# Image 0's value planes: column-mod-4 order from PSUM, eight rows at a time on ScalarE and GpSimd

## The chip, the cores and the metric

The program runs on one core of a Trainium2 chip, in one launch. Its engines are TensorE (PE, matrix products into PSUM), VectorE (DVE), ScalarE (ACT), GpSimd (POOL) and SyncE (SP, which here only issues DMAs); ACT and POOL issue some DMAs as well. PE's weight loads are listed as PEld. The metric is the device time of one execution in microseconds (us).

## The reference

The kernel computes two layers on x of shape (4, 96, 128, 128), fp32. Layer 0 is a state-space block (projection, 3x3 depthwise convolution, four scans, a norm, an output projection). Layer 1, cut to what matters:

```python
x1, x2 = split at zero and normalized from _gn(x)          # per image, 96 x 128 x 128 each
key   = conv3x3(x1, aw1);  qry = conv3x3(x2, aw2)
attn  = softmax over (c, 3x3) of the products of key and qry patches   # 96 x (96*9) per image
value = conv3x3(x1, aw3)
y1    = layer_norm(conv3x3(value, attn))                   # each image has its own filter attn
y2    = layer_norm(conv3x3(x2, w_conv2)) * x1
x     = x + xr + conv1x1(concat(y1, y2), w_full) + b_full
```

## The kernel before

The program is emitted by Python generators that run in pairs: co_run steps a left generator and a right one, at a given ratio of their costs. A scheduler then places the instructions on the engines' queues; each engine and each DMA queue works through its own list in order.

The order of stages: projections and scans of all four images; from about 2550 us on, beside the rest of the scan, image 0's convolutions (direct_maps); from about 3290 us on, when the scan has ended, the same convolutions beside image 1's norm and split; then the attention of images 0 to 3, each beside the norm and split of the next image and the output of the last one.

**The convolutions of image 0** (direct_maps, pair_sets). They work on plain rows, three at a time, in bank-sized PSUM tiles of psl (three of them). There are 22 strips of six rows; in each, m = 0 makes key and value from x1d, m = 1 makes query and the other convolution from x2d. For each m, two chunks of three rows give 128 output channels (96 of key or query, and 32 of the value or other), and one product of 2 x 64 channels the rest. convolve evicts each PSUM tile with ACT copies (L2116). The 32 channels go to the ring and from there to DRAM (last_32, L1783); the 64 channels go to the tile value or o and from there to DRAM (first_64, L1800). For m = 0 the DRAM tensor is vd, rows of 129 columns with a leading zero.

**Image 0's value planes.** The attention multiplies transformed inputs: each row is cut in tiles of four columns, and six linear combinations of six neighbouring columns make the planes vp. For images 1 to 3 the value is made in column-mod-4 order on the chip. For image 0, lift reads rows of vd back (L2143) into a padded tile and pixel_planes makes the planes on DVE: 12 instructions per four rows (L1428 to L1437) with steps of four columns. store_planes writes them to vp (L1444). lift is called after every strip with the number of rows that are surely there, and makes at most four lifts then; once more with all rows after the attention's weights are made:

```python
for _ in range(4 if rows < H else H // LR):
    a = lifted[0]
    if not img.lifting or a + LR > rows:
        return
```

img.lifting becomes true when the scan has ended.

**The other helper for planes.** planes_of serves images whose rows lie in column-mod-4 order, 33 places for each of the four residues (PP = 132 a row, the last place of each zero). With vector=True it works on DVE (L1380 to L1387, and L1373); otherwise ACT makes two scaled copies x4 and x2 (L1394, L1395), and POOL ten sums and differences (L1403 to L1408, and four of L1373). Image 1's split uses both forms, one for x1p and one for x2p, after DVE's selection L1230 of what ACT scaled (L1226).

**Image 1's norm** (ssm_output, 16 steps). It runs on all engines beside the convolutions: PE L950 and L1002 into banks of psr (two of them), DVE L1015 and L1021, POOL L1016, two small DMAs in POOL's queue (L988 writes a row rd, L996 spreads it out as r).

**After the convolutions.** Taps.weights makes the softmax (L1692, L1694), PE transposes it (L1703), DVE copies it (L1704) and transforms the filter (L1265 to L1271); it is stored as watd and read back as wa by ACT's queue (L1337 to L1343). Attention.load reads ya and yc from the planes (L1880, L1888), ACT copies parts as yb (L1905), and products multiplies them (L1471).

Of the kernel before, what the change touches and what calls it, by code (L numbers as in the profile page):

```python
# [9 lines left out]
F32 = mybir.dt.float32  # L10
BF16 = mybir.dt.bfloat16
AF = mybir.ActivationFunctionType
ALU = mybir.AluOpType
# [4 lines left out]
C = 96  # L18
# [16 lines left out]
PP = PB * TW  # L35
AA = 2.0
AR = 12
LR = 4
GROUP = 9
NG = H // GROUP  # L40
NSTRIP = (H + AR - 1) // AR
# [28 lines left out]
def kernel(  # L70
# [1168 lines left out]
    def turned_view(v):  # L1239

        return v.rearrange("p (h t j) -> p h j t", t=TN, j=TW)
# [101 lines left out]
                eng.dma_start(w3[p : p + 32, j], wd[64:96, 2, i])  # L1343
        return w1, w2, w3

    def padded(t, r):


        v = t[:, : r * PP].rearrange("p (h w) -> p h w", w=PP)
        nc.gpsimd.memset(v[:, :, W + 1 : PP], 0.0)  # L1350
        nc.gpsimd.memset(v[:, :, 0:1], 0.0)
        nc.gpsimd.memset(t[:, r * PP :], 0.0)
        return v[:, :, 1 : W + 1]

    def planes_of(later, pool, t, r, then, most=RS, vector=False, bufs=2, p=C):


# [52 lines left out]
            later(lambda: then(pl), 2)  # L1410

        return at_once if vector else scaled

    def pixel_planes(later, pool, t, r, then):

        v = t[:, : r * PP].rearrange("p (h x) -> p h x", x=PP)

        def x(k):  # L1420
            return v[:, :, k : k + W - TW + 1 : TW]

        def made():
            f = pool.tile([C, 6, r, TN], F32, name="diff", bufs=1)
            pl = pool.tile([C, NP, r * TN], F32, name="pl")
            stt = nc.vector.scalar_tensor_tensor
            for k in range(TW):
                stt(f[:, k], x(k), -AA * AA, x(k + 2), ALU.mult, ALU.add)  # L1428
            for k in (1, 2):
                nc.vector.tensor_sub(f[:, 3 + k], x(k + 2), x(k))  # L1430
            to = [pl[:, i].rearrange("p (h t) -> p h t", t=TN) for i in range(NP)]
            nc.vector.tensor_sub(to[0], f[:, 2], f[:, 0])
            nc.vector.tensor_sub(to[5], f[:, 3], f[:, 1])
            nc.vector.tensor_add(to[1], f[:, 2], f[:, 1])
            nc.vector.tensor_sub(to[2], f[:, 2], f[:, 1])
            for i, a in ((3, AA), (4, -AA)):
                stt(to[i], f[:, 4], a, f[:, 5], ALU.mult, ALU.add)  # L1437
            later(lambda: then(pl))

        return made  # L1440

    def store_planes(eng, m, r0, r, pl):
        to = m[:, :, r0 + 1 : r0 + 1 + r].rearrange("c i h t -> c i (h t)")
# [129 lines left out]
    def by_threes(v, r):  # L1573

        return v.rearrange("p (i q) w -> p i q w", q=min(3, r))
# [191 lines left out]
                    lambda ks=ks, groups=groups: self.multiplied(s == 0, ks, *groups)  # L1767
                )

    def last_32(img, m, v, c0, r, k):  # L1770

        r0, r = r

        def f():
            if m:
                for i in range(v.shape[1]):
                    nc.vector.bn_stats(img.c2a[96:128, k + i], v[96:128, i])
                to = img.c2d[64:96, r0 * W : (r0 + r) * W]
            else:
                to = img.vd[64:96, (r0 + 1) * PW : (r0 + 1 + r) * PW]  # L1780
            to = to.rearrange("c (h w) -> c h w", h=r)
            for i in range(v.shape[1]):
                nc.sync.dma_start(to[:, 3 * i : 3 * i + v.shape[2]], v[96:128, i])  # L1783

        return f

    def first_64(img, m, t, parts, chunks, k):


        def f():  # L1790
            if m:
                for p, e, v, _ in parts:
                    for i in range(v.shape[1]):
                        nc.vector.bn_stats(img.c2b[p:e, k + i], v[:, i])
            for q, (r0, r) in enumerate(chunks):
                if m:
                    to = img.c2d[0:64, r0 * W : (r0 + r) * W]
                else:
                    to = img.vd[0:64, (r0 + 1) * PW : (r0 + 1 + r) * PW]
                nc.sync.dma_start(to, t[64 * q : 64 * q + 64, : to.shape[1]])  # L1800

        return f

    def pair_sets(img, taps, later, pool, rows, inputs, convolve, lift):

        value = pool.tile([128, rows * PW], F32, name="value", bufs=1)
        nc.gpsimd.memset(value.rearrange("p (h w) -> p h w", h=rows)[:, :, 0:1], 0.0)
        c = 0  # L1810
        per = rows // 3
        for s, chunks in enumerate(strips_of(rows)):
            for m in (0, 1):
                read = []
                for q, (r0, r) in enumerate(chunks):
                    read.append(inputs(c, q))
                    c += 1
                    jobs = [(0, 128, 0, read[q], r * W)]
                    to = [(0, 128, taps.rows(m, r0, r, 1), r)]
                    v = taps.rows(m, r0, r, 1 if m else 0)  # L1820
                    then = last_32(img, m, v, 0, (r0, r), per * (2 * s + q))
# [6 lines left out]
                v = t.rearrange("p (h w) -> p h w", h=rows)  # L1828
                if not m:
                    v = v[:, :, 1:PW]  # L1830
                rs = [r for _, r in chunks]
                if rs == [rows, rows]:
                    to = [(0, 128, by_threes(v, rows), rows)]
                else:
                    to = [
                        (64 * i, 64 * i + 64, by_threes(v[64 * i : 64 * i + 64, :r], r), r)
                        for i, r in enumerate(rs)
                    ]
# [220 lines left out]
    def direct_maps(img, ps):  # L2059
# [3 lines left out]
        with (  # L2063
# [32 lines left out]
            def convolve(jobs, m, to, then):  # L2096
                pc = bank(ps)
                for i, (k, d) in enumerate(terms):
                    for p, e, c, t, n in jobs:
                        v = t[k][:, d : d + n // W * PW].rearrange("p (h w) -> p h w", w=PW)  # L2100
                        w = ws[m][k][:, d] if k < 2 else ws[m][2]
                        nc.tensor.matmul(  # L2102
                            pc[p:e, :n].rearrange("p (h w) -> p h w", w=W),
                            lhsT=w[:, c : c + e - p],
                            rhs=v[:, :, 0:W],
                            start=(i == 0),
                            stop=(i == len(terms) - 1),
                        )
                    if i in (2, 4, 6):
                        later.tick()  # L2110
                        yield 2.1 if i == 2 else 1.4

                def out():
                    for p, e, v, r in to:
                        of = pc[p:e, : r * W].rearrange("p (h w) -> p h w", w=W)
                        nc.scalar.copy(v, by_threes(of, r))  # L2116
                    later(then)

                later(out)
# [8 lines left out]
            def lift(rows):  # L2128
# [5 lines that stand above are left out]
                    if not lifts:  # L2134
                        lifts.append(
                            pools.enter_context(tc.tile_pool(name="lifts", bufs=2, side="left"))
                        )
                    lifted[0] = a + LR
                    h = lifts[0].tile([C, LR * PP + 4], F32, name="lift")
                    to = padded(h, LR)  # L2140
                    src = img.vd[:, (a + 1) * PW : (a + LR + 1) * PW]
                    src = src.rearrange("c (h w) -> c h w", w=PW)
                    nc.sync.dma_start(to, src[:, :, 1:PW])  # L2143
                    later(pixel_planes(
                        later, lifts[0], h, LR, lambda pl, a=a: store_planes(nc.sync, img.vp, a, LR, pl)
                    ), 2)
                    yield 1.2

# [303 lines left out]
    with tc.tile_pool(name="wp", bufs=1, side="left") as wp:  # L2452
# [7 lines left out]
        for images, pace in (([0], 0.25), ([1], 0.75), ([2, 3], 1.35)):  # L2460
            left = projections(images, weights, stats, wp, psl)
            if images[0] == 0:
# [3 lines left out]
                next(made)  # L2466
                while ready[0] < 2:
                    next(left)
                maps = [new_map(n) for n in ("x1d", "x2d", "vd")]
                planes = [  # L2470
                    [new_planes(f"{n}{i}") for n in ("x1p", "x2p", "vp")] for i in range(2)
                ]
# [154 lines left out]
```

## Time and profile before

| what | value |
|---|---|
| runs of the kernel | 6656.29 us median of three, 6639.72 to 6660.51 |
| the profiled execution | 6633.8 us; span from the first to the last instruction 6631.9 us |
| mean granted TensorE clock | 0.886 |
| busy share of the span | PE 81%, PEld 35%, DVE 74%, ACT 57%, POOL 53% |
| instructions | 76453 |

A busy share is an average over stages that have different limits, so the stages around the change are to be read one by one. In the views, "<-" in front of a name says what an idle engine was waiting for; an entry such as "DVE diff L1430" names the engine, the tile and the line. Groups give the count after x, the busy us, the mean ns of one, and the idle time before. A view of one tile gives the shortest, median and longest duration in ns and the first and last start in us.

### The profile page before, as it was taken

Reading aid. Unit: us, or ns where it says so; the run is one execution under the profiler, and the core shown is the slowest. Engines: PE = TensorE matmul, PEld = TensorE weight load, DVE = VectorE, ACT = ScalarE, POOL = GpSimd, SP = SyncE. Lnnn points to the kernel's source line nnn. Section 1 sums busy time; section 2 is a strip of 40 time slices with the busy share of each in tenths; the row PEclk is TensorE's granted clock in tenths of the full one; section 3 lists DMA queues with packets and bytes.
Section 4 is the critical chain, followed back from the end, with each engine's and each line's share of the span. In section 5 each row is a group of like instructions: output and inputs, shape, how many; then the busy total and the mean of one; then the engine's idle time right before and its main releaser. Section 6 shows DMA issues by size and latency. Waiting matters only on the chain. (4 is left out here: it accounts for less than half of the span.)

```text
span 6631.9 us, 76453 instructions
## 1 busy us (share of the span) xinstructions
PE 5374.8 (81%) x23264; PEld 2337.9 (35%) x23264; DVE 4907.7 (74%) x7469; ACT 3803.6 (57%) x4751; POOL 3506.9 (53%) x2744
## 2 busy tenths in 40 slices
PE   5889988987887736989987479877888777887988
PEld 2333323322222102444433134444333444344553
DVE  3247778988997568989755885588875788898666
ACT  1257768777786566676534464475544654545542
POOL 2236758978787436969621354466234574034320
PEclk9999989998997757999998789987988887998989
DMA  7766777866765667665666765655775555866547
GB/s 165 174 155 181 201 206 198 223 192 163 222 182 162 187 171 213 198 199 170 203 184 177 195 182 156 174 143 157 206 202 155 147 154 154 227 173 188 150 122 213
DMA packets 888487, 1198.29 MB, mean 181 GB/s; under 512 B 216143, under 2 KB 741015, under 8 KB 875597
## 3 DMA queue, kind: packets, MB, share of 16 engines
q1 hardware_dynamic: 864460, 1138.46, 63.1%
q0 software_dynamic: 16208, 38.42, 2.2%
q10 hardware_dynamic: 7408, 16.53, 0.8%
q8 instruction: 187, 3.06, 0.2%
q14 instruction: 224, 1.83, 0.1%
HBM read 777.62 MB, written 345.58 MB: 169 GB/s over the span
## 5 line engine op out<-in xcount | busy, mean ns | idle before, releaser
L622 PE MATMUL bank<-y,wp 128*128 128x512 f32 (+3 forms) x3584 | 1316.6, 624 | 85.5 <-DMA y<-y 34.4
L855 POOL TENSOR_TENSOR y<-y,dl 128x1024 f32<-128x1024 f32 x384 | 1056.4, 2751 | 272.1 <-DVE dl L847 238.0
L822 POOL TENSOR_TENSOR dl<-dl,u 128x1024 f32<-128x1024 f32 x384 | 1009.2, 2628 | 223.6 <-ACT dA L798 107.5
L843 DVE TENSOR_TENSOR_SCAN dA<-dA,pBC 128x512 f32<-128x512 f32 x768 | 981.5, 1278 | 30.7
L1471 PE MATMUL two<-ya,wd 128*64 128x192 f32 (+3 forms) x2376 | 595.1, 427 | 193.5 <-ACT odd L1542 96.8
L847 DVE TENSOR_TENSOR dl<-dA,pBC 128x512 f32<-128x512 f32 x768 | 528.0, 688 | 271.4 <-PE pBC L736 198.5
L736 PE MATMUL pBC<-xr,wbc 60*128 60x512 bf16 (+1 forms) x1536 | 458.8, 403 | 330.0 <-DVE dA L843 257.7
L622 PEld LDWEIGHTS bank<-y,wp 128*128 128x128 f32 (+3 forms) x3584 | 458.8, 169 | 754.2 <-issue 655.5
L2102 PE MATMUL bank<-y,wn 128*128 128x384 f32 (+5 forms) x2408 | 676.8, 504 | 43.0 <-DMA y<-x2d 18.9
L1905 ACT COPY yb<-ya 64x768 f32<-64x768 f32 (+1 forms) x660 | 537.8, 815 | 152.0 <-PE two L1471 111.7
L665 ACT ACTIVATE dl<-pd,dtb 128x512 f32<-128x512 f32 x768 | 485.6, 684 | 181.2 <-PE pd L736 171.3
L1471 PE MATMUL two<-yb,wd 128*64 128x192 f32 (+3 forms) x2376 | 567.6, 411 | 21.3 <-ACT yb L1905 21.3
L826 DVE TENSOR_TENSOR pBC<-dl,pBC 128x512 f32<-128x512 f32 x768 | 527.5, 687 | 9.7 <-POOL dl L822 8.8
L2102 PEld LDWEIGHTS bank<-y,wn 128*128 128x128 f32 (+3 forms) x2408 | 307.5, 167 | 338.9 <-issue 165.4
L798 ACT ACTIVATE dA<-dl,negA 128x1024 f32<-128x1024 f32 x384 | 420.3, 1141 | 2.3
L1471 PEld LDWEIGHTS two<-ya,wd 128*64 128x64 f32 (+1 forms) x2376 | 268.9, 172 | 405.4 <-ACT odd L1542 104.0
L736 PEld LDWEIGHTS <-wbc 60*128 60x128 bf16 (+1 forms) x1536 | 103.4, 96 | 767.7 <-issue 754.0
L665 ACT ACT_TABLE_LOAD x245 | 314.3, 1283 | 100.9 <-PE pd L736 93.6
L1975 POOL COPY own<-ring 32x512 f32<-32x512 f32 (+1 forms) x198 | 225.3, 1172 | 260.7 <-DVE ring L1564 224.4
L1471 PEld LDWEIGHTS two<-yb,wd 128*64 128x64 f32 (+1 forms) x2376 | 294.0, 173 | 167.5 <-issue 37.3
L2209 POOL MEMSET o<- 1x1024 f32 x60 | 56.3, 946 | 560.3 <-PE bank L2264 225.3
L1471 PE MATMUL two<-ya,wa 128*96 128x384 f32 (+1 forms) x528 | 230.1, 519 | 123.3 <-DMA ya<-vp 82.5
(323 smaller groups left out, 9936.6 us busy)
## 6 DMA issues: line engine op xcount, KB each, us to landing
u<-zb SPq DMA_DIRECT2D x192, 1024.0 KB
yms<-y SPq DMA_DIRECT2D x96, 512.0 KB
y<-yms SPq DMA_DIRECT2D x64, 768.0 KB
xn<-xnew SPq DMA_DIRECT2D x128, 384.0 KB
ya<-vp SPq DMA_DIRECT2D x120, 336.0 KB
y<-y SPq DMA_DIRECT2D x128, 258.2 KB
zb<-z SPq DMA_DIRECT2D x64, 512.0 KB
ya<-x1p SPq DMA_DIRECT2D x90, 336.0 KB
```

The source lines that it names most:

```text
L622: nc.tensor.matmul(blocks(pz[p:e]), lhsT=ws[k][:, d, c : c + e - p], rhs=window(ys[k], at, d, n), start=(i == 0), stop=(i == len(terms) - 1),)
L665: nc.scalar.activation(dst, src, AF.Softplus, bias=bias)
L736: nc.tensor.matmul(p, lhsT=w[rows], rhs=xr[rows, at : at + CH], start=True, stop=True)
L798: nc.scalar.activation(live[m]["dA"], live[m]["dl"], AF.Exp, scale=negA[:, g % 3, k : k + 1])
L822: nc.gpsimd.tensor_mul(t, t, u_view(n))
L826: nc.vector.tensor_mul(p, live[n]["dl"][:, bass.ts(half, CH)], p)
L843: nc.vector.tensor_tensor_scan(h, h, p, init, ALU.mult, ALU.add)
L847: nc.vector.tensor_mul(live[n]["dl"][:, sl], live[n]["dA"][:, sl], live[n]["C", half])
L855: nc.gpsimd.tensor_add(v, v, t.rearrange("p (a b) -> p a b", b=W))
L1471: nc.tensor.matmul(of(to[p:e], r), lhsT=w[:, i, c : c + e - p], rhs=tiles(t[k][PAIR[i]][:, SLOT[i]], o, r), start=(k == 0), stop=False,)
L1905: nc.scalar.copy(yb[k][64 * h - 64 : 64 * h, :, :n], ya[k][0:64, :, h * TN : h * TN + n])
L2102: nc.tensor.matmul(pc[p:e, :n].rearrange("p (h w) -> p h w", w=W), lhsT=w[:, c : c + e - p], rhs=v[:, :, 0:W], start=(i == 0), stop=(i == ...
```

## The change

The value of image 0 leaves PSUM in column-mod-4 order. The 96 query or key channels are evicted as before, and for m = 0 the 32 value channels get an ACT copy of their own into one of two places of a new tile, whose borders are cleared once; the 64 channels go in the same order to the tile value. vd becomes rows of 132 places with the borders in them, so each store is one run per channel. lift reads eight rows (LR = 8) as one run per channel and calls planes_of in its ACT and POOL form with one buffer each for x4, x2 and the planes; pixel_planes and padded go.

```diff
-LR = 4
+LR = 8
...
+    def turned_rows(t, r):
+        return t[:, : r * PP].rearrange("p (h j b) -> p h j b", j=TW, b=PB)[:, :, :, 0:TN]
...
     def last_32(img, m, v, t, r, k):
...
             if m:
...
             else:
+                nc.sync.dma_start(
+                    img.vd[64:96, r0 * PP : (r0 + r) * PP], t[:, : r * PP]
+                )
...
-        value = pool.tile([128, rows * PW], F32, name="value", bufs=1)
+        value, end = (
+            pool.tile([128, rows * PP], F32, name=f"value{i}", bufs=1) for i in range(2)
+        )
+        ends = end[96:128], end[64:96]
...
-                    to = [(0, 128, taps.rows(m, r0, r, 1), r)]
+                    if m:
+                        to = [(0, 128, v, r)]
+                    else:
+                        to = [(0, 96, v[0:96], r), (96, 128, turned_rows(ends[q], r), r)]
...
-                        of = pc[p:e, : r * W].rearrange("p (h w) -> p h w", w=W)
-                        nc.scalar.copy(v, by_threes(of, r))
+                        of = pc[p:e, : r * W]
+                        if list(v.shape[2:]) == [TW, TN]:
+                            of = turned_view(of)
+                        else:
+                            of = by_threes(of.rearrange("p (h w) -> p h w", w=W), r)
+                        nc.scalar.copy(v, of)
...
-                    h = lifts[0].tile([C, LR * PP + 4], F32, name="lift")
-                    to = padded(h, LR)
-                    src = img.vd[:, (a + 1) * PW : (a + LR + 1) * PW]
-                    src = src.rearrange("c (h w) -> c h w", w=PW)
-                    nc.sync.dma_start(to, src[:, :, 1:PW])
-                    later(pixel_planes(
-                        later, lifts[0], h, LR, lambda pl, a=a: store_planes(nc.sync, img.vp, a, LR, pl)
+                    h = lifts[0].tile([C, LR * PP], F32, name="lift")
+                    nc.sync.dma_start(h, img.vd[:, a * PP : (a + LR) * PP])
+                    later(planes_of(
+                        later, lifts[0], h, LR,
+                        lambda pl, a=a: store_planes(nc.sync, img.vp, a, LR, pl), LR, bufs=1,
                     ), 2)
...
-                maps = [new_map(n) for n in ("x1d", "x2d", "vd")]
+                maps = [new_map(n) for n in ("x1d", "x2d")]
+                maps.append(dram.tile([C, H * PP], F32, name="vd", bufs=1))
```

The helper that is called now, in the form that lift takes:

```python
def scaled():
    x4 = pool.tile([p, most * PP], F32, name="x4", bufs=bufs)[:, : r * PP]
    x2 = pool.tile([p, most, 2, PB], F32, name="x2", bufs=1)[:, :r]
    nc.scalar.mul(x4, t[:, : r * PP], a2)
    nc.scalar.mul(x2, v.rearrange("p h (k b) -> p h k b", b=PB)[:, :, 0:TW:2], AA)
    later(lambda: differences(x4.rearrange("p (h x) -> p h x", x=PP), x2))
```

More of the change, by code (lines that the diff above doesn't have):

```diff
@@ L1344, in product_stack @@
         return w1, w2, w3
[L1346 to L1353, printed above, removed]
     def planes_of(later, pool, t, r, then, most=RS, vector=False, bufs=2, p=C):
@@ L1412, in planes_of @@
         return at_once if vector else scaled
[L1414 to L1440, printed above, removed]
     def store_planes(eng, m, r0, r, pl):
@@ L1768, in complete, with last_32 @@
                 )
-    def last_32(img, m, v, c0, r, k):
+    def turned_rows(t, r):
+        return t[:, : r * PP].rearrange("p (h j b) -> p h j b", j=TW, b=PB)[:, :, :, 0:TN]
+    def last_32(img, m, v, t, r, k):
         r0, r = r
@@ L1775, in f @@
             if m:
+                to = img.c2d[64:96, r0 * W : (r0 + r) * W].rearrange("c (h w) -> c h w", h=r)
                 for i in range(v.shape[1]):
                     nc.vector.bn_stats(img.c2a[96:128, k + i], v[96:128, i])
-                to = img.c2d[64:96, r0 * W : (r0 + r) * W]
+                    nc.sync.dma_start(to[:, 3 * i : 3 * i + v.shape[2]], v[96:128, i])
             else:
[L1780 to L1783, printed above, removed]
+                nc.sync.dma_start(
+                    img.vd[64:96, r0 * PP : (r0 + r) * PP], t[:, : r * PP]
+                )
         return f
@@ L1795, in f @@
             for q, (r0, r) in enumerate(chunks):
[L1796 to L1800, printed above, removed]
+                to, n = (img.c2d, W) if m else (img.vd, PP)
+                nc.sync.dma_start(
+                    to[0:64, r0 * n : (r0 + r) * n], t[64 * q : 64 * q + 64, : r * n]
+                )
         return f
     def pair_sets(img, taps, later, pool, rows, inputs, convolve, lift):
-        value = pool.tile([128, rows * PW], F32, name="value", bufs=1)
-        nc.gpsimd.memset(value.rearrange("p (h w) -> p h w", h=rows)[:, :, 0:1], 0.0)
+        value, end = (
+            pool.tile([128, rows * PP], F32, name=f"value{i}", bufs=1) for i in range(2)
+        )
+        ends = end[96:128], end[64:96]
+        for t in (value, end):
+            nc.gpsimd.memset(t, 0.0)
         c = 0
@@ L1818, in pair_sets @@
                     jobs = [(0, 128, 0, read[q], r * W)]
-                    to = [(0, 128, taps.rows(m, r0, r, 1), r)]
-                    v = taps.rows(m, r0, r, 1 if m else 0)
-                    then = last_32(img, m, v, 0, (r0, r), per * (2 * s + q))
+                    v = taps.rows(m, r0, r, 1)
+                    if m:
+                        to = [(0, 128, v, r)]
+                    else:
+                        to = [(0, 96, v[0:96], r), (96, 128, turned_rows(ends[q], r), r)]
+                    then = last_32(img, m, v, ends[q], (r0, r), per * (2 * s + q))
                     yield from convolve(jobs, m, to, then)
@@ L1827, in pair_sets @@
                 t = pool.tile([128, rows * W], F32, name="o3") if m else value
[L1828 to L1838, printed above, removed]
+                to = []
+                for i, (_, r) in enumerate(chunks):
+                    v = t[64 * i : 64 * i + 64]
+                    if m:
+                        v = by_threes(v[:, : r * W].rearrange("p (h w) -> p h w", w=W), r)
+                    else:
+                        v = turned_rows(v, r)
+                    to.append((64 * i, 64 * i + 64, v, r))
+                if [r for _, r in chunks] == [rows, rows]:
+                    if m:
+                        v = by_threes(t.rearrange("p (h w) -> p h w", w=W), rows)
+                    else:
+                        v = turned_rows(t, rows)
+                    to = [(0, 128, v, rows)]
                 rest = convolve(jobs, m, to, first_64(img, m, t, to, chunks, per * s))
@@ L2114, in out @@
                     for p, e, v, r in to:
-                        of = pc[p:e, : r * W].rearrange("p (h w) -> p h w", w=W)
-                        nc.scalar.copy(v, by_threes(of, r))
+                        of = pc[p:e, : r * W]
+                        if list(v.shape[2:]) == [TW, TN]:
+                            of = turned_view(of)
+                        else:
+                            of = by_threes(of.rearrange("p (h w) -> p h w", w=W), r)
+                        nc.scalar.copy(v, of)
                     later(then)
```

## The prediction

> **What bounds the kernel now.** The page's slices come first. In its second part TensorE (PE) is busy 7 to 9 tenths almost everywhere; slice 23 of 40 (3647 to 3813 us) falls to 4. That is where image 0's value planes are finished, so I cut this stretch into stages. The columns are stage, length, busy us and count of PE, weight loads, DVE, ACT and POOL, granted clock, DMA share, GB/s.
>
> ```profile
> 3290.00:3570.00 280.00, 246.09 (x932) 96.72 (x931) 134.71 (x352) 85.23 (x122) 71.65 (x120) 0.95 0.68 181
> 3570.00:3638.00 68.00, 39.68 (x164) 25.31 (x163) 39.89 (x119) 47.05 (x85) 0.98 (x15) 0.75 0.69 180
> 3638.00:3722.00 84.00, 1.49 (x9) 1.20 (x8) 83.49 (x227) 20.11 (x28) 32.71 (x63) 0.50 0.62 165
> 3722.00:3890.00 168.00, 138.74 (x472) 58.70 (x473) 146.71 (x243) 117.22 (x154) 64.76 (x83) 0.92 0.81 220
> 3890.00:4604.00 714.00, 574.02 (x3461) 321.04 (x3457) 502.06 (x930) 391.06 (x542) 405.63 (x511) 0.87 0.58 154
> ```
>
> Between 3638 and 3722 PE has nothing to do for over 80 us, while DVE works 83.49 of 84 us. The timeline of PE says what ends the gap:
>
> ```profile
> 3637.61 1.64 PE L1703 MATMUL bank<-ident,sm 96*96 96x96 f32 x9 [5.37 <-DVE sm L1694]
> 3721.76 1.57 PE L1471 MATMUL two<-ya,wa 128*96 128x384 f32 x2 [82.51 <-DMA ya<-vp]
> ```
>
> The attention of image 0 starts when its first planes (ya, read from vp) arrive. Their load is behind the last plane store in SP's queue, as the timeline of SP shows:
>
> ```profile
> 3714.35 0.56 SPq L1444 DMA_DIRECT2D vp<-pl  x1
> 3714.96 2.21 SPq L1343 DMA_DIRECT2D wd<-wd  x4
> 3717.62 1.77 SPq L1880 DMA_DIRECT2D ya<-vp  x4
> ```
>
> The groups of DVE in 3636 to 3721 us tell what it does meanwhile:
>
> ```profile
> L1428 DVE SCALAR_TENSOR_TENSOR diff<-lift 96x128 f32<-96x128 f32 x48 | 18.6, 439 | 0.0
> L1230 DVE SCALAR_TENSOR_TENSOR half<-xn,kept,bank 96x512 f32<-96x512 f32 x16 | 11.2, 736 | 0.1
> L1430 DVE TENSOR_TENSOR diff<-lift 96x128 f32<-96x128 f32 x24 | 8.5, 391 | 0.0
> L1437 DVE SCALAR_TENSOR_TENSOR pl<-diff 96x128 f32<-96x128 f32 x24 | 8.2, 380 | 0.0
> L1435 DVE TENSOR_TENSOR pl<-diff 96x128 f32<-96x128 f32 x12 | 4.8, 398 | 0.0
> ```
>
> With L1432 to L1434 (3.6, 4.2, 3.9 us) the lines of pixel_planes make 51.8 us for 12 lifts of four rows. So 12 of the 32 lifts are left over for a time when nothing else feeds PE, and DVE is the **bound of the gap**.
>
> **What the Trainium skill says.** "GPSIMD Engine Reference", section "3.1 Elementwise", has a two-input fp32 operation about twice as slow on GpSimd as on VectorE. The trace agrees: a plane of 256 elements takes 0.79 us on POOL (L1373, below) and 0.40 to 0.42 us on DVE. "SBUF — State Buffer", section "Who interferes with whom", says that GpSimd and a VectorE operation with two SBUF inputs exclude each other for a whole instruction. It agrees too: four L1428 took 3.25 us at 3649.42, beside planes on POOL, and 1.25 us at 3655.47 without. "DMA: Bandwidth & Descriptors", section "Anatomy of one DMA", puts some 2 us fixed on a DMA from GpSimd's queue; here rd<-mq of 4 KB took 2.8 us and r<-rd of 384 KB took 5.1 us (medians).
>
> **The change part by part.** (1) *Planes leave DVE.* 128 L1428, 64 L1430, 64 L1437 and 4 x 32 others go: 44.4+23.5+17.8+38.7 = 124 us by the groups of 3290 to 3720 us. Instead each lift of eight rows costs two ACT operations and ten on POOL. The rows of the same helper on image 1's split, in the gap, give their price:
>
> ```profile
> L1373 POOL TENSOR_TENSOR pl<-x x12: 769/791/1187, 3648.2 to 3689.8; 96x256 f32<-96x256 f32 x12
> L1394 ACT ACTIVATE x<-half x4: 1066/1066/1067, 3644.0 to 3717.8; 96x1056 f32<-96x1056 f32 x4
> L1395 ACT ACTIVATE x<-half x4: 638/640/640, 3644.9 to 3718.8; 96x528 f32<-96x528 f32 x4
> L1403 POOL TENSOR_TENSOR x<-half,x x4: 1095/1321/1848, 3645.1 to 3718.9; 96x528 f32<-96x528 f32 x4
> L1404 POOL TENSOR_TENSOR x<-half,x x3: 1106/1142/1146, 3646.3 to 3684.3; 96x512 f32<-96x512 f32 x3
> ```
>
> POOL: 1.32+1.14+0.64+0.77+0.74+0.83+4x0.79 = 8.6 us a lift, 138 us for 16; 96 small memsets (0.1 us) go. ACT: 1.7 us a lift, 27 us.
>
> (2) *Eight rows a lift.* A call of lift makes at most four lifts, and lifting starts when the scan has ended, with five calls left (row limits 102, 108, 114, 120, 126). Before: 5 x 4 x 4 = 80 rows, so 48 rows, 12 lifts, remain for lift(H). After: 32, 64, 96, then three lifts to 120; **one lift** of eight rows remains. This is what empties the gap, more than the change of engine.
>
> (3) *The gap.* What must still follow the last convolution: row 127's store to vd (issued 3622 to 3623), its lift's load (about 3630), ACT 1.7, POOL 8.6, store and load of planes with some 3 us each to land: about 3655 us. Beside it run the softmax weights. L1694 ends at 3637.5. In the changed program DVE has after it only four L1230 (2.8 us), three L1704 (1.3), the filter transform (9 us as it ran: L1265 to L1271) and one vector half of a split piece (5 to 6 us): some 18 us, about 3656. The store of watd and its reload took 3678.62 to 3683.29 before the first wa load was issued, 4.7 us; the loads and two yb copies 5 to 7 us more. So PE restarts at about **3668 instead of 3721.8: -54 us** (3660 to 3690: -62 to -32). SP's queue loses 12 loads (0.32) and 12 stores (0.56) here; its first ya load now stands behind image 1's first x1p and x2p stores, which end at about the same 3656.
>
> (4) *Work moved behind the gap.* In the gap DVE also did 16 L1230 and four pieces of the split's vector half. The shorter gap holds about two pieces less on DVE, at some 5 to 7 us each. They then run in stages where DVE is busy 147 of 168 and 502 of 714 us. About half shows: **+6 us** (0 to 15).
>
> (5) *POOL in the stage 3290 to 3570.* It is busy 72 of 280 us; 15 lifts make it 72+129, about 200. Nothing else is moved off it but memsets. What it delays:
>
> ```profile
> L1016 POOL TENSOR_TENSOR r<-r,xr 96x512 f32<-96x512 f32 x32 | 51.8, 1627 | 60.3 <-DVE r L1015 42.1 <-ACT xr L1048 10.0 <-DVE mq L970 6.5
> L996 POOL DMA_DIRECT2D r<-rd x16 | 8.4, 526 | 36.4 <-DMA rd<-mq 22.5 <-issue 7.8 <-DMA xnew<-r 3.8
> L988 POOL DMA_DIRECT2D rd<-mq x16 | 8.4, 525 | 64.9 <-DVE mq L981 62.8 <-DMA xnew<-r 1.9 <-issue 0.2
> ```
>
> Image 1's norm sends two small DMAs through POOL's queue in each of 16 steps of 17.5 us. A lift that stands between L988 and L996 makes r up to 8.6 us later. DVE's L1015 waited for r 25.1 us in five cases already, so on DVE there is no slack; PE waits only when both banks of psr are taken ("PE bank L950 <- DVE r L1015" is 10.4 us in all). In about half the steps a large part of a lift lies between the two; I take half of those to hit PE with 4 us: **+15 us** (-5 to +45; below nothing because POOL's memsets waited for DVE at the head of this queue, and those waits go).
>
> (6) *ACT.* 43 row blocks of value get a second eviction of 32 partitions: L2116's 0.48 us, 21 us in all, read from PSUM with a step of four. No row shows that step for this copy; I take the same 0.48, between 0.4 and 0.8. Most run from 2560 to 3290, where PE is the bound (180 of 190 us in its last part) and three banks cover them; a conv matmul that waits for its bank sees up to 0.5 us each. An L1394 that waits for its load, or for the single x4 buffer until POOL is through, holds the evictions queued behind it on ACT; ACT is busy 85 of 280 us. **+4 us** (0 to 10). The stores to vd become contiguous runs; the DMA share of 0.6 to 0.7 hides that: nothing.
>
> Sum: -54+6+15+4 = **-29 us** against the profiled execution's 6633.8 us (span 6631.9): 6605. That execution lies 22 us under the median of the runs, 6656, to which the forecast refers: **6627 us**. Some 0.3% (20 us) is what a measurement of this kernel can tell from no change.
>
> **The rivals.** *POOL becomes the bound* (slower): r late holds PE behind two banks. The other terms leave 44 us of gain, so it decides from 2.9 us of PE time per lift in 15 lifts; with the 6 us that a lift in the way costs r, 90 us are lost: +46, 6702. For it speaks DVE's lack of slack, against it PE's 12 us of convolution between its uses of the banks, where I looked (3445 to 3457 us). *The weights end the gap* (no change): wa's loads were all issued only at 3694.97, partly for want of freed space. If that stays and PE restarts at 3697, the gain is 25 us, and (4) to (6) take it back: 6656. *No giving back* (faster): -54, 6602. *The lifts don't catch up*: the row limits above fix them, so only late execution on POOL could do it; that is the first rival.
>
> **How the numbers follow.** The forecast with its milder and stronger forms has 0.62, no change 0.22, the slower rival 0.16. The range 6585 to 6672 goes from a gap of 32 us less, fully given back with 16 us more, to the full gain and (5) at its lower end.
>
> **What would show it.** Right: PE's gap after the last transposes under 40 us; one lift after the weights; DVE's lines of lift gone and POOL's busy time up by 120 to 140 us; waits of PE for L1015 in the norm stage under 25 us. Wrong: a gap of over 60 us, or the norm stage over 300 us.

## The result, and the profile after

The changed kernel takes 6684.3 us (median of seven runs, 6668.3 to 6697.1) against 6655.2 us (seven runs of the kernel before). The ratio is **1.0047, with a 95% interval of 1.0029 to 1.0065: slower**, where 6627 us and faster was forecast. The profiled execution took 6690.2 us (span 6688.4). It is 56.4 us longer than the one of before, while the medians differ by only 29 us: the profiled one of before was 21 us under its median and this one 6 us over. Gaps of 10 us between two profiles therefore prove little by themselves.

The busy times of the engines over the whole execution, after:

```profile
PE 5432.7 (81%) x23264; PEld 2359.3 (35%) x23264; DVE 4821.3 (72%) x7085; ACT 3847.9 (58%) x4826; POOL 3613.4 (54%) x2809
```

The amounts of work moved as computed. By the groups of the whole trace, the DVE lines of pixel_planes are gone (-124.4 us), the sums on POOL have grown by 120.8 us (7.6 us a lift; 8.6 were forecast), the two scalings on ACT by 27.8 us (27), and the evictions on ACT by 20.0 us (21).

The stages, cut where they end now (columns as in the prediction: stage, length, PE, weight loads, DVE, ACT, POOL, clock, DMA share, GB/s):

```profile
3290.00:3570.00 280.00, 224.65 (x784) 84.84 (x786) 89.19 (x130) 96.12 (x135) 142.40 (x175) 0.87 0.61 167
3570.00:3694.00 124.00, 79.88 (x300) 41.80 (x297) 51.23 (x120) 66.67 (x116) 40.96 (x54) 0.79 0.61 162
3694.00:3719.00 25.00, 0.83 (x6) 0.51 (x4) 21.71 (x40) 5.23 (x8) 15.06 (x18) 0.50 0.67 188
3719.00:3890.00 171.00, 142.48 (x470) 59.64 (x472) 146.15 (x246) 119.12 (x157) 66.74 (x86) 0.89 0.85 230
```

The gap has shrunk from 84 to 25 us, as forecast. But it begins 56 us later: in the first 280 us PE issues 784 matmuls where it issued 932, and the rest fills another 124 us. PE's timeline around the gap:

```profile
3693.19 1.65 PE L1666 MATMUL bank<-ident,sm 96*96 96x96 f32 x9 [9.94 <-DVE sm L1657]
3719.23 1.56 PE L1434 MATMUL two<-ya,wa 128*96 128x384 f32 x2 [24.39 <-DMA wa<-watd]
```

PE restarts at 3719.2 us; before it was 3721.8. The gap now ends with the weights (wa) and no longer with the planes (ya). In SP's timeline, the last lift is read and its planes are stored, and then the loads of ya follow:

```profile
3678.30 0.38 SPq L2119 DMA_DIRECT2D lift<-vd  x1
...
3691.99 0.60 SPq L1407 DMA_DIRECT2D vp<-pl  x1
...
3713.78 2.39 SPq L1855 DMA_DIRECT2D ya<-vp  x4
```

Where the 56 us went is seen in ACT's timeline. L943 starts image 1's norm, L1110 is the first step after it. First the kernel before, then the changed one:

```profile
3296.96 1.06 ACT L943 ACTIVATE sq<-y 96x1024 f32<-96x1024 f32 x1 [3.67 <-DMA y<-yms]
3577.02 1.23 ACT L1110 ACTIVATE xr<-xn,shift,rstd 96x1024 f32<-96x1024 f32 x1
```

```profile
3290.79 1.06 ACT L943 ACTIVATE sq<-y 96x1024 f32<-96x1024 f32 x1 [3.64 <-DMA y<-yms]
3636.65 1.24 ACT L1110 ACTIVATE xr<-xn,shift,rstd 96x1024 f32<-96x1024 f32 x1
```

Image 1's norm lasts 346 us instead of 280. The convolutions stand beside it in PE's queue, and the last one ends at 3680.9 us instead of 3627.6. The norm of image 2 begins at 4057.3 instead of 4020.9 us, that of image 3 at 4939.2 instead of 4897.7, and the end is 56 us later.

What DVE waits for between 3290 and 3640 us (us, times, longest), the changed kernel:

```profile
DVE mq L969 <- DMA mq<-st: 57.4, 11, 11.9
DVE xstats L1021 <- POOL r L1016: 48.5, 24, 9.9
DVE r L1015 <- DMA r<-rd: 33.6, 5, 11.8
DVE r L1015 <- PE bank L1002: 24.9, 8, 8.4
```

L1021 waits 48.5 us for the addition on POOL (28.3 before). And one group has grown where nothing was changed. L969 squares 8 rows of 128 numbers; 16 of them took 6.2 us before:

```profile
L969 DVE TENSOR_TENSOR mq<-mq 8x128 f32<-8x128 f32 x16 | 21.1, 1320 | 57.4 <-DMA mq<-st 57.4
```

One of them shows why. DVE's timeline, and under it POOL's:

```profile
3320.81 6.30 DVE L969 TENSOR_TENSOR mq<-mq 8x128 f32<-8x128 f32 x1 [1.07 <-DMA mq<-st]
3327.15 0.28 DVE L970 TENSOR_TENSOR mq<-mq 8x128 f32<-8x128 f32 x1
```

```profile
3320.65 1.08 POOL L1395 TENSOR_TENSOR x<-lift,x 96x512 f32<-96x512 f32 x1
3321.70 0.72 POOL L1397 TENSOR_TENSOR x<-x 96x256 f32<-96x256 f32 x1
...
3325.05 1.23 POOL L1364 TENSOR_TENSOR pl<-x 96x256 f32<-96x256 f32 x2
3326.25 0.72 POOL L1397 TENSOR_TENSOR x<-x 96x256 f32<-96x256 f32 x1
3327.86 1.09 POOL L1394 TENSOR_TENSOR x<-lift,x 96x528 f32<-96x528 f32 x1 [0.90 <-ACT x L1385]
```

An operation of 0.28 us lasts 6.30 us. It ends when POOL's unbroken run of sums does (3326.97 us), at the first pause of 0.90 us. L969 heads the row statistics L970, L971, L981, L988, on which each of the norm's 16 steps depends.

Holds as long as this are seen in this one profile. In those of p4 and q4 below, where POOL makes the same sums, the 16 take 5.4 and 7.3 us, and these kernels lose 0.34 and 0.46% all the same. So the holding of L969 is not the main cost.

The DMA that ends the row statistics waits too. L981 gives the row that L988 sends, and L988 stands in POOL's queue. First DVE, then POOL, in one step of the changed kernel:

```profile
3465.23 0.94 DVE L981 RECIPROCAL mq<-mq 8x128 f32<-8x128 f32 x1 [1.46 <-ACT mq L975]
```

```profile
3466.69 0.64 POOL L1396 TENSOR_TENSOR pl<-lift 96x256 f32<-96x256 f32 x1 [0.91 <-DMA vp<-pl]
...
3471.32 1.52 POOL L1016 TENSOR_TENSOR r<-r,xr 96x512 f32<-96x512 f32 x1
3472.78 0.53 POOL L988 DMA_DIRECT2D rd<-mq  x1
```

The row is ready at 3466.18 us, and L988 is issued 6.61 us later, after seven sums of a lift and one L1016. Over the 16 steps of the norm these waits make 21.6 us, against 5.9 us before.

### The profile page after: what moved, and what is told of

The parts are those of the page before. It is cut to its first block, busy times and chain, and to the rows that moved or that the text cites. A ratio compares the mean times of both kernels' runs of the same rounds, so it can differ in the third digit from the quotient of the medians.

```text
span 6688.4 us, 76081 instructions
## 1 busy us (share of the span) xinstructions
PE 5432.7 (81%) x23264; PEld 2359.3 (35%) x23264; DVE 4821.3 (72%) x7085; ACT 3847.9 (58%) x4826; POOL 3613.4 (54%) x2809
## 5 line engine op out<-in xcount | busy, mean ns | idle before, releaser
L855 POOL TENSOR_TENSOR y<-y,dl 128x1024 f32<-128x1024 f32 x384 | 1057.7, 2754 | 268.7 <-DVE dl L847 230.4
L1434 PE MATMUL two<-ya,wd 128*64 128x192 f32 (+3 forms) x2376 | 606.0, 431 | 210.0 <-ACT odd L1505 102.0
L2077 PE MATMUL bank<-y,wn 128*64 128x384 f32 (+5 forms) x2408 | 683.8, 508 | 48.4 <-DMA y<-x1d 18.3
L1434 PE MATMUL two<-yb,wd 128*64 128x192 f32 (+3 forms) x2376 | 580.4, 415 | 23.6 <-ACT yb L1880 23.6
L2077 PEld LDWEIGHTS bank<-y,wn 128*64 128x64 f32 (+3 forms) x2408 | 311.8, 169 | 346.6 <-issue 179.6
L1434 PEld LDWEIGHTS two<-ya,wd 128*64 128x64 f32 (+1 forms) x2376 | 272.2, 173 | 417.7 <-ACT odd L1505 109.4
L1434 PEld LDWEIGHTS two<-yb,wd 128*64 128x64 f32 (+1 forms) x2376 | 300.0, 174 | 177.8 <-issue 50.0
L1364 POOL TENSOR_TENSOR pl<-x 96x256 f32<-96x256 f32 (+2 forms) x520 | 347.0, 682 | 0.0
```

The lines of the kernel that those rows point to most:

```text
L855: nc.gpsimd.tensor_add(v, v, t.rearrange("p (a b) -> p a b", b=W))
L1434: nc.tensor.matmul(of(to[p:e], r), lhsT=w[:, i, c : c + e - p], rhs=tiles(t[k][PAIR[i]][:, SLOT[i]], o, r), start=(k == 0), stop=False,)
L2077: nc.tensor.matmul(pc[p:e, :n].rearrange("p (h w) -> p h w", w=W), lhsT=w[:, c : c + e - p], rhs=v[:, :, 0:W], start=(i == 0), stop=(i == ...
```

## The experiments

All the kernels in one table. The times are from one profile each, in us: the norm's length (first L943 to first L1110), then three moments counted from the start of the scan's last L855: the start of the last matmul of image 0's convolutions, PE's restart with the attention, and the first L943 of image 2's norm. The ratio is that of the runs to the kernel before on the same chip.

| kernel | norm | last conv | restart | norm 2 | ratio (95%) |
|---|---|---|---|---|---|
| before | 280 | 342 | 436 | 735 | 1 |
| after | 346 | 401 | 440 | 778 | 1.0047 (1.0029 to 1.0065) |
| e1 lifts on DVE | 319 | 371 | 415 | 750 | 0.9997 (0.9987 to 1.0007) |
| e2 before, eight rows | 308 | 360 | 410 | 746 | 0.9995 (0.9984 to 1.0006) |
| e3 after, four rows | 283 | 353 | 472 | 765 | 1.0030 (1.0016 to 1.0044) |
| e4 sums on DVE | 316 | 371 | 410 | 747 | 1.0011 (1.0000 to 1.0022) |
| p1 before, half pace | 292 | 340 | 426 | 751 | 1.0030 (1.0018 to 1.0042) |
| p2 before, catch-up | 306 | 384 | 422 | 735 | 0.9985 (0.9971 to 0.9999) |
| p3 e1, full pace | 311 | 390 | 436 | 745 | 1.0015 (1.0005 to 1.0025) |
| p4 after, full pace | 321 | 400 | 444 | 755 | 1.0034 (1.0022 to 1.0046) |
| q1 after, L1016 on DVE | 319 | 374 | 415 | 746 | 1.0015 (1.0007 to 1.0023) |
| q2 e1 + idle sums | 362 | 417 | 465 | 798 | 1.0091 (1.0078 to 1.0104) |
| q3 before, double pace | 272 | 351 | 467 | 716 | 1.0038 (1.0026 to 1.0050) |
| q4 four rows, catch-up | 331 | 413 | 457 | 772 | 1.0046 (1.0031 to 1.0061) |
| s1 q2, L1016 on DVE | 341 | 397 | 445 | 781 | 1.0054 (1.0037 to 1.0071) |
| s2 e1, L1016 on DVE | 303 | 353 | 397 | 732 | 0.9985 (0.9973 to 0.9997) |
| s3 four rows on DVE, catch-up | 314 | 391 | 438 | 748 | 1.0006 (0.9996 to 1.0017) |

### Which part of the change costs it: e1 to e4

e1, the lifts in the helper's DVE form:

```diff
-  lambda pl, a=a: store_planes(nc.sync, img.vp, a, LR, pl), LR, bufs=1,
+  lambda pl, a=a: store_planes(nc.sync, img.vp, a, LR, pl), LR, bufs=1, vector=True,
```

> Everything as in the changed kernel (value in column-mod-4 order, eight rows a lift), but the lifts' planes are made by the same helper in its VectorE form, so ScalarE and GpSimd have nothing of them. Theory (the ten sums on GpSimd, standing between L988, L996 and L1016, lengthen image 1's norm from 280 to 346 us, and that delay lasts to the end): image 1's norm, first L943 to first L1110, returns to 280 to 295 us, GpSimd's busy time falls by about 130 us, and the time is 6620 to 6645 us. Rival 'the burst' (stores and loads of eight rows in SP's queue) and rival 'the pace' (16 lift steps of 1.2 in place of 32 let image 1's work be emitted later): nothing of either changes, so the norm stays above 330 us and the time at about 6680. Rival 'the evictions' (43 more ScalarE copies): as the burst, above 330 us and 6680.

Measured: 6648.7 us, 0.9997. The whole loss is gone, so ACT and POOL as the lifts' engines are what made the change slower. But the norm is still 319 us, not 280 to 295, and there is no gain: something else eats what the shorter gap brings.

e2, the kernel before with LR = 8:

```diff
-LR = 4
+LR = 8
```

> The kernel before with LR = 8 alone: pixel_planes on VectorE, no column-mod-4 order of the value, no lift on GpSimd. Theory (GpSimd): the norm stays at 280 to 295 us, the gap of TensorE after the last transposes shrinks from 82 to 25 to 40 us, and the time is 6620 to 6650 us. Burst and pace: they are both in this kernel, so the norm is longer, 320 to 346 us, and the time is 6670 to 6690. Evictions: they are not in it, norm 280, 6620 to 6650 as the theory.

Measured: 6651.1 us, 0.9995; norm 308, restart 26 us earlier than before. No clear case for either side: eight rows alone lengthen the norm by 28 us, without POOL, layout or evictions, and cost nothing in the end. The earlier restart is given back.

e3, the changed kernel with LR = 4:

```diff
-LR = 8
+LR = 4
```

> The changed kernel with LR = 4: ScalarE and GpSimd make the planes, four rows at a time, 20 lifts before the attention's weights and 12 after them. Theory (GpSimd): in the norm GpSimd has 20 lifts of about 4.6 us, 92 us in place of 129, so the norm is about 325 us; the 12 lifts that are left, some 55 us of GpSimd, come after the last convolution, so TensorE's gap is 60 to 85 us and the time 6685 to 6710. Pace: 32 lift steps again, so the norm is back at 280 to 300 us, the gap as before, the time about 6655. Burst: four rows again, the same as pace.

Measured: 6673.0 us, 1.0030. The theory's norm of 325 us did not come: it is 283 us, although POOL is busy 133 us in it (71 before): POOL's busy time alone doesn't make the norm long. Here the loss lies where 12 lifts on POOL follow the last convolution: the restart is 36 us later.

e4, the ten sums on DVE, the two scalings still on ACT:

```diff
-  lambda pl, a=a: store_planes(nc.sync, img.vp, a, LR, pl), LR, bufs=1,
+  lambda pl, a=a: store_planes(nc.sync, img.vp, a, LR, pl), LR, bufs=1, eng=nc.vector,
...
-  sub, add = nc.gpsimd.tensor_sub, nc.gpsimd.tensor_add
+  sub, add = eng.tensor_sub, eng.tensor_add
...
-  sums(nc.gpsimd, mid, outer, to)
+  sums(eng, mid, outer, to)
```

> The changed kernel with the ten sums of each lift on VectorE in place of GpSimd; ScalarE still makes x4 and x2 into single buffers. Theory (GpSimd's queue): the norm returns to 280 to 300 us, the time to 6620 to 6650. Rival 'ScalarE held by its single buffers' (x4 and x2 of the next lift wait for the sums, with evictions and L1048 behind them): VectorE frees them sooner but the wait stays in kind, so the norm stays at 320 us or more and the time at 6670 or more. Pace, burst, evictions: norm above 330 us, 6680.

Measured: 6657.7 us, 1.0011; norm 316, about as in e1 and between both expectations. ACT's single buffers are not the main cause; some 0.14% (1.0011 to 0.9997) may be ACT's part, and the two intervals overlap.

### What eats the gain of eight rows: p1 to p4, q3

The number that a lift yields tells co_run how far to run image 1's work. Half as many lifts mean half as many steps, and image 1's norm and split are emitted later; in the program's order on PE, image 2's norm then stands behind 384 attention products instead of 348 (L1434, the product of a ya and that of its yb counted as one). The forecast had not looked at this.

p1 changes only that number in the kernel before; p3 and p4 set it to 2.4 in e1 and in the changed kernel, q3 to 2.4 in the kernel before:

```diff
-                    yield 1.2
+                    yield 0.6
```

> The kernel before with one number changed: the lift step yields 0.6 in place of 1.2. No lift, size or engine changes; co_run only steps image 1's norm and split 16 x 1.2 = 19 units less while the 32 lifts are emitted, which is just what eight rows a lift do, and image 2's norm then stands behind 36 more attention products on TensorE. Pace theory (the eight-row step costs by this what its shorter gap gains): norm of image 1 295 to 310 us, norm of image 2 starts 10 to 30 us later than the 4020.9 of before, gap still about 80 us, time 6665 to 6685 us. Rival 'catch-up' (the norm is longer because 12 more lifts of work stand beside it): nothing of that here, so norm 280 us, time 6651.

Measured: 6665.8 us, 1.0030; norm 292 us, norm 2 starts 16 us later. So in the kernel before halving the pace costs 0.3% by itself.

p2, the kernel before with the catch-up alone:

```diff
-                for _ in range(4 if rows < H else H // LR):
+                for _ in range(8 if rows < H else H // LR):
```

> The kernel before with up to 8 in place of 4 lifts a call, four rows each, on VectorE: the lifts catch up with the strips as in the eight-row kernel, with 32 steps of 1.2, so the pace stays. Pace theory: the norm stays at 280 to 290 us, TensorE restarts at about 3690 and not 3722, image 2's norm starts no later than before, time 6615 to 6640 us. Catch-up theory: norm 305 to 320 us as with eight rows, and time 6650.

Measured: 6639.4 us, 0.9985. With the pace kept there is a gain, but of 0.15% only. The norm is 306 us (the catch-up theory's number) and the last convolution 42 us later than before: DVE's lifts, brought forward out of the gap, lengthen the stage into which they go. PE restarts 14 us earlier, not 54.

> The changed kernel with the lifts' planes on VectorE (as in the first experiment) and a step of 2.4 for each lift of eight rows, which gives image 1's work the pace of before. Pace theory: norm 280 to 295 us, restart about 3690, image 2's norm at 4020 or earlier, time 6615 to 6635. Rival (eight-row bursts or the column-mod-4 evictions cost the norm, or the clock does): as without the step, 6649, norm about 315.

Measured: 6655.3 us, 1.0015. The pace theory misses: norm 2 starts 5 us earlier than in e1, but the last convolution is 20 us and the restart 22 us later, and the time is 0.18% longer.

> The changed kernel, lifts on ScalarE and GpSimd, with the step of 2.4 alone. The two causes add: the pace gives back what it costs (about 20 to 28 us of the norm), GpSimd's share stays (about 28 us of the norm, 30 us of the time against the VectorE form). So norm 305 to 325 us, time 6650 to 6668. If GpSimd's share comes only with the late pace, norm 280 to 295 and 6620 to 6640; if the pace costs nothing, 6684.

Measured: 6663.7 us, 1.0034, norm 321: inside what the adding of two causes gives. But the interval overlaps that of the changed kernel, and in p3 the same step made the lifts on DVE slower and not faster, so this hit does not show that the two causes add.

> The kernel before with a step of 2.4 in place of 1.2 for each lift, so that image 1's norm and split are emitted earlier against the convolutions; nothing else changes, and image 2's norm stands behind 72 fewer attention products. Half the pace cost 18 us. If the end follows the start of the next images' norms: that start moves 10 to 25 us forward and the time is 6625 to 6640. If the pace of before is the best, because work emitted earlier only crowds the convolutions: 6650 to 6665.

Measured: 6666.7 us, 1.0038. Norm 2 starts 19 us earlier, as expected, and the time is longer, since PE restarts 31 us later. So my second theory, that image 1's norm and split alone are the path, falls too. What fits p1 and q3 is that two strands end at about the same time, the attention of one image and the norm and split of the next, so that moving one ahead by holding back the other loses. Of the three steps tried, 1.2 is the best in the kernel before.

### How GpSimd costs it: q1, q2, q4, s1, s2, s3

q1, the changed kernel with image 1's addition on DVE:

```diff
-  nc.gpsimd.tensor_add(v, v, turned_view(xr))
+  (nc.vector if b == 1 else nc.gpsimd).tensor_add(v, v, turned_view(xr))
```

> The changed kernel with L1016 (the addition of image 1's norm) on VectorE instead of GpSimd; the lifts stay on ScalarE and GpSimd. In the changed kernel VectorE's L1021 waits 48.5 us for L1016 in the norm stage. If GpSimd's share comes from the addition standing behind the lifts' sums, the norm falls from 346 to 320 to 330 us and the time from 6684 to 6660 to 6672. If it comes from the two small DMAs of GpSimd's queue (L988, L996) standing behind the sums, or from the late planes, the norm stays above 338 us and the time at 6678 to 6690.

Measured: 6656.6 us, 1.0015, norm 319: two thirds of what e1 regains (0.32 of 0.50%). The norm pays for L1016 on POOL. How much of this is for standing behind the sums is not settled: the same move brings s2, below, 0.12% over e1 where no sums are ahead of L1016.

The forecast had named the small DMAs. From the issue of L988 to that of L996 a step takes 7.7 us in the changed kernel, 7.8 in e1 and 8.2 in q1 (5.1 before), so a lift standing between the two does not tell these kernels apart. But the wait of L988 behind L981 does: 21.6 us over the 16 steps in the changed kernel, 11.0 in q1, 5.6 in e1. This DMA has a part in the loss, and no run separates it from L1016's.

q2, e1 with ten sums for each lift on POOL whose results are not used:

```diff
+  sub(s, v[:, :, 2 * PB :], v[:, :, : 2 * PB])
+  sub(s[:, :, : 2 * TN], v[:, :, 1 : 1 + 2 * TN], v[:, :, 2 * PB : 2 * PB + 2 * TN])
+  for _ in range(8):
+      sub(s[:, :, :TN], v[:, :, 3 * PB : 3 * PB + TN], v[:, :, PB : PB + TN])
```

> The first experiment's kernel (lifts on VectorE, 6649 us) with ten more GpSimd operations for each lift, of the same sizes and also reading the lift's rows, whose results nobody uses (one more tile is written, nothing else changes). GpSimd theory (its queue is what is lost): norm 335 to 346 us in place of 319, time 6670 to 6685. Rival 'late planes or ScalarE' (what costs is that the planes are ready later, or ScalarE's copies): norm 315 to 325, time 6649.

Measured: 6702.3 us, 1.0091, norm 362. No result of these sums is used, and yet they cost 0.94% over e1, more than expected. So time on POOL costs. Not all of it is time in POOL's queue, though, for the sums also read the lift's tile, of which there are two, and keep it. SP's queue waits for them before it loads the next lift, 45.3 us in six cases, where in e1 these loads wait for DVE alone (29.3 us):

```profile
SPq L2128 <- POOL beside L2114: 45.3, 6, 11.8
```

Late lifts, and whatever stands behind their loads in SP's queue, are therefore not ruled out. The excess was the question for s1 and s2.

s1 is q2, s2 is e1, both with the edit of q1.

> The kernel with lifts on VectorE and ten idle sums on GpSimd for each lift (6702 us), with L1016 on VectorE in addition, so that of image 1's norm only L988 and L996 stand in GpSimd's queue. If the idle sums cost by the addition behind them: the time falls by 25 to 45 us, to 6657 to 6677, norm 320 to 335. If they cost by slowing VectorE (L1364 on it was 0.56 in place of 0.46 us) or by the small DMAs behind them, the time stays within 15 us of 6702.

> Lifts on VectorE and L1016 on VectorE too, no idle sums: GpSimd has nothing of image 1's norm but two DMAs a step. Against the same kernel with L1016 on GpSimd (6649) this shows what L1016 costs on GpSimd when nothing stands before it. Theory (it was the queue, not the engine): the same or a little slower, 6645 to 6662. If GpSimd's 1.6 us against VectorE's some 0.8 us counts by itself: 6625 to 6640.

Measured: s1 6680.8 us, 1.0054; s2 6639.0 us, 0.9985. Both miss the theory: s1 falls between its two expectations, and s2 into the second one, in which L1016 costs on POOL by itself. Taking it out of the queue brings 0.37% beside the idle sums and 0.12% without them; the intervals of e1 and s2 overlap, so the 0.12% is not clear of noise.

The idle sums cost 0.69% even where no addition stands behind them (s1 against s2). Three things differ there. L988 waits 47.6 us behind L981 in s1 and 5.0 in s2, much like the difference of the norms (341 and 303 us). SP's queue waits 41.0 us for the idle sums before loads of lifts. And DVE is slower. How the 0.69% is split among them is open. For the third, DVE's groups of one plane line, 3290 to 3660 us, in s2 (no elementwise work of norm or lifts on POOL), e1 (L1016 on POOL) and q2 (L1016 and idle sums):

```profile
L1364 DVE TENSOR_TENSOR plv<-diff 96x256 f32<-96x256 f32 x64 | 23.0, 409 | 0.0
```

```profile
L1364 DVE TENSOR_TENSOR plv<-diff 96x256 f32<-96x256 f32 x60 | 24.3, 455 | 0.0
```

```profile
L1364 DVE TENSOR_TENSOR plv<-diff 96x256 f32<-96x256 f32 x56 | 28.2, 556 | 0.0
```

The same instruction takes 0.41, 0.46 and 0.56 us, and what differs beside it is what POOL does. In s1, where L1016 is on DVE too, POOL's 528-element sums take 1.57 us (1.20 in q2). So both engines lose where both make sums.

q4 is the changed kernel with LR = 4 and the 8 of p2 in the loop; s3 is e1 with both.

> The changed kernel with four rows a lift and up to eight lifts a call: ScalarE and GpSimd make the planes, the lifts catch up, the pace is that of before. Beside it stand the kernel before with the same eight lifts a call on VectorE (6639) and the changed kernel with the step of 2.4 (6664), whose bursts are of eight rows. GpSimd theory: the engine costs the same whatever the burst, norm about 320 us, time 6660 to 6670. If the burst of 8.6 us is what stands in the way of L988, L996 and L1016, bursts of 4.6 us cost less: norm 305 to 312, time 6640 to 6652.

Measured: 6674.3 us, 1.0046, norm 331, above both expectations. Shorter bursts don't help. Against p2, which has the rows, the catch-up and the pace in common, the new layout with ACT and POOL costs 0.61%.

> Column-mod-4 layout, lifts on VectorE of four rows, up to eight a call, 32 steps of 1.2: as the kernel before with the eight lifts a call (6639), but with the new layout and its 43 more evictions. If the layout costs nothing and saves VectorE some 20 us: 6630 to 6642. If the evictions cost what they seemed to (up to 10 us): 6642 to 6655.

Measured: 6648.2 us, 1.0006, in the second expectation. It is 0.21% over p2 (0.9985), and the two intervals just touch, so some cost of the new layout is likely. That it is the evictions' is not shown: the helper, the stores and the loads differ as well.

**The best version** is s2: the new layout, eight rows, the planes and image 1's addition on DVE. At 0.9985 it beats the kernel before by 0.15% and the changed one by more; p2 equals it.

## Why the prediction was wrong, step by step

Of the forecast's sum, -54+6+15+4 us, two terms failed above all: step (3), whose -54 us came to -2.5 us at PE's restart, and step (5), which put +15 us where image 1's norm grew by 66.

Steps (1) and (2), amounts: right. DVE, ACT and the evictions came out within 1 us of the sums, POOL 17 us under; one lift remains after the weights.

Step (3), the gap: its length right, its place wrong. It fell by 58 us (84.2 to 26.0), and -54 was forecast. But PE restarts only 2.5 us earlier, not 54. The step took row 127's store to vd at 3622 us as fixed, and with it the last convolution. That convolution ends at 3680.9 us now, 53 us later. The step failed in two ways. The lifts moved out of the gap lengthen the stage they go into: with DVE as their engine and the pace unchanged, the last convolution is 42 us later (p2). And the lifts' engines add more: 401 against 371 us (after, e1).

Step (5), POOL in the norm stage: the term that was mis-sized, +15 us (-5 to +45) where the norm grew by 66. The split by kernels: 28 to 39 us come with eight rows on DVE already (e2, e1), some 27 with POOL. The mechanism was only half right. POOL's queue does it, but in good part through L1016 (its move in q1 regains 0.32 of 0.50%), which the step showed and did not price. L988 has a part, by its wait behind L981 (21.6 us against 5.6 in e1), and not by a lift between L988 and L996. And POOL holds up DVE. The prediction quoted the Trainium skill for that, "SBUF — State Buffer", section "Who interferes with whom": each excludes the other for a whole instruction. It then priced the effect at nothing for the norm. The trace agrees and goes beyond one instruction: L969 was held through a run of them, 6.30 us for 0.28. How much of the norm this costs is not shown.

What was missing altogether: the step of a lift as a weight in co_run. Halving it costs 0.3% by itself in the kernel before (p1); p3 shows that restoring it does not give this back.

Step (4), what is given back: sized +6 us, for two pieces of DVE work. The silent assumption was that an earlier restart is worth its length at the end. It isn't: in s2 PE restarts 39 us earlier after the scan than before, norm 2 starts 3 us earlier, and the time falls by 0.15%, 10 us.

Step (6): the evictions beside the scan cost nothing that shows. The last L855 starts at 3279.6 us (3285.7 before), and over all profiles at 3279.6 to 3291.4 with the new layout and at 3283.4 to 3288.3 without it. A cost of the layout elsewhere is left open by s3.

Of the rivals, "POOL becomes the bound" was the nearest (6702 forecast, 6684 measured), and "the weights end the gap" was right as to what ends it. The sign given for the first, waits of PE for L1015 over 25 us, was a bad one: they were 12.1 us between 3290 and 3640 us. The sign that spoke was the norm stage over 300 us.

What stays open. Within the norm PE is busy 278 us for 962 matmuls at a granted clock of 0.86, before 247 us for 932 at 0.95. Busy time times clock is about 239 and 235 us, so most of the added busy time goes with the lower clock and not with more work. From 3290 to 3570 us PE issues 932, 918, 941 and 884 matmuls in before, e3, p1 and q3, at a clock of 0.95, 0.94, 0.90 and 0.89; in the kernels whose lifts catch up, leaving out those with idle sums, it issues 784 to 854, at 0.84 to 0.89. The counts do not overlap, so the lifts brought forward slow this stage; whether the clock falls because PE pauses, or PE falls behind because of the clock, was not told apart. Nor is the remaining 0.18% between q1 and e1 split: ACT, the held DVE operations, L988 and SP's queue, which waits for POOL and ACT before loads and stores of lifts, are all candidates.

## What to carry to other kernels

Before moving sums from VectorE to GpSimd, list what GpSimd has to do in the same stretch for a chain with a deadline, the DMAs in its queue included, and the two-input operations of VectorE beside them: a GpSimd that was busy only 71 of the norm's 280 us was not free for them here. Work moved out of a gap is not gone; price it in the stage where it lands, and ask whether a second strand ends at the same time before counting the gap as gain. Where generators are interleaved by costs, a change in how many steps one makes is a change of the schedule, and can be tried alone.

## What the runs showed of the hardware that I had not expected

A small two-input VectorE operation can be held through a whole run of back-to-back GpSimd operations and not just one: 6.30 us at 3320.81 us in the changed kernel, against 0.28 us when undisturbed. It got through at GpSimd's first pause, here one of 0.90 us. Two more cases took 4.04 us at 3419.81 us and 2.05 us at 3461.15 us, and ended just after GpSimd had gone over to issuing a DMA (L996, at 3423.41 and 3463.01 us). It is no rule: at 3508.15 and 3544.05 us the same operation took 1.09 and 0.79 us and ended between two GpSimd sums that followed each other without a pause. What decides between the two is not shown.
